# A transformer block's first image: LN1 tokens kept in the large buffers, weights loaded behind the first tokens and prepared in two stages, and a new order of the instructions

## The chip, the core and the metric

The kernel runs on one core of a Trainium2 chip. A core has five engines with an instruction queue each: TensorE (PE, matrix products and transposes), VectorE (DVE), ScalarE (ACT), GpSimd (POOL) and SyncE (SP, which here only issues transfers). Each works through its own queue in order; they wait for each other by semaphores. Transfers (DMA) are issued from the queues of SP, ACT and POOL. Data lie in SBUF (128 partitions) and, for PE's results, in eight PSUM banks. The metric is the device time of one execution in microseconds (us).

## What is computed

Sixteen images of 128 channels, 96 x 96 pixels, float32, go through one block: a layer norm over channels (LN1), channel attention with 8 heads, a residual sum, a second layer norm (LN2) and a feed-forward part with a depthwise 3x3 convolution, and a second residual sum. The reference, cut to what matters:

```python
xn1 = _layernorm(x_hwc, ln1_w, ln1_b)
q, k, v = xn1 @ wq.T, xn1 @ wk.T, xn1 @ wv.T         # 8 heads of 16 channels
q, k = _l2norm(q), _l2norm(k)                          # over all 9216 pixels
attn = softmax(einsum('bhcn,bhdn->bhcd', q, k) * 16 ** -0.5)
x = x + (attn applied to v) @ wp.T
xn2 = _layernorm(x, ln2_w, ln2_b)
h1 = einsum('bchw,oc->bohw', xn2, w_in)                # 128 -> 512 channels
h2 = depthwise_conv3x3(h1, w_dw)
x = x + einsum('bchw,oc->bohw', gelu(h2), w_out)       # 512 -> 128
```

## The kernel before

**Tiling.** An image is cut into 8 bands of 12 rows and 24 units of 4 rows (384 pixels). A band of x (128 channels x 1152 pixels) is one buffer of the pool `xb` or `x1`. Normalising needs pixels on partitions: 128 pixels form a tile, four tiles a *quad*; an image has 18 quads.

**LN1 and the Gram matrix** (`norm`, with `second` false). For each quad PE transposes four tiles (`forth`, line 602) into a PSUM bank (`h` for the first image, `tr` else), DVE takes their statistics (line 609), POOL computes variance plus epsilon (616) and its power -1/2 (620), and the tokens are scaled into a buffer `zT` (634 by DVE for half of the first image's tiles, 647 by ACT). There are three `zT` buffers, each with a column of ones. From `zT` PE sums the Gram matrix of the image (`gram`, 661) and transposes back to channels (`back`, 692, one bank `pB`), and ACT copies the result into a padded buffer `xn` (`place`, 698). A `zT` buffer is free for a later quad when its Gram product and its transposes back are done.

**Attention** (`attention`) works on the 128 x 128 Gram matrix alone: a chain of small steps on PE (764 to 846), DVE, POOL (810) and ACT (exp at 825), whose last result is one matrix `mwT`. PE then multiplies the normalised image by it (`mix`, 560), and x is added, by DVE (`residual`, 566) for the first image's first bands and otherwise by ACT (569) and an accumulating transfer (572).

**LN2** is `norm` again with `second` true: transposes (602), statistics, variance, power, the shift `nb` on DVE (624), scaling (638, 651), transposes back and place (696, with border rows at 702).

**Feed-forward.** For each band and each chunk of 128 hidden channels PE computes `hidden` (877), ACT copies it out (`kept`, 882), and the nine taps of the convolution are shared: ACT multiplies two or three taps into `pr` buffers (890) that accumulating transfers add (899), DVE does the others (895). For chunk 3 of about half the bands PE does the convolution as nine matmuls (945). Gelu follows on ACT (903, 951), then the output matmuls (968), DVE's sum (975) and the store (979). The large buffers `h3` (ten of them, 128 x 1152) hold the convolution's results; at the start two of them hold the raw weights.

**Weights** (`weights`). One step issues five loads on ACT's queue (417 to 421) into two `h3` buffers. PE transposes and DVE scales them into their final places: first those of attention (432 to 467), then the others (`winT`, `woutT`, `comp`).

**The order** is not written by hand. Every step is handed to `Plan.op` with its engine, an assumed duration, what it reads and writes, and a *place*, which is a position on the time line in units of feed-forward jobs plus an offset from the table `AT`, by kind of step. `Plan.order` plays the queues through with the assumed durations: when an engine is idle it takes, of the steps whose inputs are ready and whose buffers are free, that with the smallest place. The resulting sequence is what the program contains; on the chip each engine runs its part of it in that fixed order. Buffers of the pools in `IN_TURN` are given out in order of place. `T_ADD`, `T_MOVE` and `T_WEIGHTS` are the assumed durations of transfers; they act through the order alone.

Of the kernel before, what the change touches and what calls it, by code (L numbers as in the profile page):

```python
# [9 lines left out]
F32 = mybir.dt.float32  # L10
# [8 lines left out]
BR = 12  # L19
# [13 lines left out]
AT = dict(  # L33
    weights=86, zeros=34, load_a=-17.95, forth_a=-1.35, stats_a=-23.85, variance_a=50.15, power_a=-16.45,
    scaled_a=6.1, gram=-31.8, back_a=-145.85, place_a=68, attention=-19.55, mix=-17.6, residual=60.15,
    mixed=-98.2, add_x=-22.85, forth_b=-2, stats_b=-5.55, variance_b=52.05, power_b=-11, shift_b=-76.95,
    scaled_b=98.5, back_b=-23.15, place_b=20.55, halo=21.65, hidden=1.35, kept=-79.55, products=8.4,
    add_last=-64.4, tap=0.1, add_first=-14.5, gelu=-63.5, conv=1.15, conv_gelu=-1.85, out=4.9, add=-43.45,
    store=47.1,
)  # L40
# [4 lines left out]
WAIT = dict(POOL=350, SP=1300, ACT=1300)  # L45
T_WEIGHTS = 20000
T_VARIANCE = 420
T_POWER = 1000
T_ADD, T_MOVE = 3100, 1800

# [156 lines left out]
def tile_restormer_block(  # L207
# [138 lines left out]

    def at(kind, place):
        return place + AT[kind]

# [21 lines left out]
    def pe(ns, p, f, r, w):  # L371
        op("PE", ns, p, f, r, w, ns + 200 + SLACK, ns)
# [32 lines left out]
    def weights(p):  # L405
# [16 lines left out]

        def transposed(parts, kept, gives):

            key = ("weights", next(names))
            h = ("h", key)
            d = {}

            def forth():
                d["pt"] = bank(key)  # L430
                for k, part in enumerate(parts()):
                    nc.tensor.transpose(d["pt"][:, k * P : (k + 1) * P], part, ident)

            pe(440, at("weights", p), forth, mine, [h])
            dve(700, at("weights", p), lambda: kept(d["pt"]), [h], [("w", g) for g in gives] + mine[1:])

# [55 lines left out]
        def unit_parts():  # L492
            for n in range(NCH):
                nc.vector.tensor_scalar(v["wt"][:, n, :], v["win"][:, n, :], unit[:, n : n + 1], None, ALU.mult)

        op("ACT", 400, at("load_a", p), loads, [], mine, T_WEIGHTS, dma=2 * T_MOVE)
        dve(1400, at("weights", p), units, [], [("w", "in")])
        dve(400, at("weights", p), shifts, [], [("w", "in"), ("w", "conv"), ("w", "shift")])
        transposed(
            lambda: [v["wqk"][:, :P], v["wqk"][:, P:], v["wp"], wv_sb], keep_qkp, ["qk"]  # L500
        )
# [4 lines left out]
        dve(800, at("weights", p), keep_centred, [pc], [("w", "qk")])  # L506
        dve(700, at("weights", p), unit_parts, [mine[0], ("w", "in")], [mine[1]])
        transposed(
            lambda: [v["wt"][:, n, :] for n in range(NCH)],
            lambda pt: nc.vector.tensor_scalar(winT.rearrange("p n c -> p (n c)"), pt, w2, None, ALU.mult), ["in"],  # L510
        )
        transposed(
            lambda: [v["wout"][:, n * P : (n + 1) * P] for n in range(NCH)],
            lambda pt: nc.vector.tensor_copy(woutT.rearrange("p n c -> p (n c)"), pt), ["out"],
        )
        for t0 in (0, 4, 8):
            ts = range(t0, min(t0 + 4, 9))
            dve(170 * len(ts), at("weights", p), lambda ts=ts: comp_parts(ts), [mine[0]], [mine[1]])
            transposed(
                lambda ts=ts: [v["wt"][:, t % 4, :] for t in ts],  # L520
                lambda pt, ts=ts: nc.vector.tensor_scalar(
                    comp[:, ts[0] : ts[-1] + 1, :].rearrange("p t c -> p (t c)"), pt[:, : len(ts) * P],
                    w2, None, ALU.mult,
                ), ["conv"],
            )
# [18 lines left out]
    def norm(i, second, place_of):  # L544
# [8 lines left out]
        def x2(s, u):  # L553
# [22 lines left out]
            if loaded:  # L576
                pe(t_mm(UT), at("mix", s), mix, [*ins, xtok(u)], [pm])
                dve(t_dve(UT), at("residual", s), residual, [pm], [xtok(u)])
                return
            pe(t_mm(UT), at("mix", s), mix, ins, [pm, xtok(u)])  # L580
            act(t_act(UT, 1) - 43, at("mixed", s), mixed, [pm], [xtok(u)])
            if u % UPB == UPB - 1:
                xb = [xtok(b * UPB + k) for k in range(UPB)]
                add(at("add_x", s), add_x, [], xb)

        def pixels(s, m):
# [4 lines left out]
            key_ = "h" if early else "tr"  # L591
            by_dve = QT // 2 if early else 0

            def forth(q):
# [31 lines left out]
            def zT(q):  # L626
                zTs[q] = zT_bufs[plan.slot["zT", (name, q)]]
                return zTs[q]
# [38 lines left out]
            for q, tr in zip(qs, trs):  # L667
                units = {t // TPU: None for t in range(q * QT, (q + 1) * QT)}
                pe(110 * QT, at("forth" + ab, s), lambda q=q: forth(q), [xtok(u) for u in units], [tr])
            for j in range(QB * QT // 2):  # L670
                dve(341, at("stats" + ab, s), lambda j=j: stats(j), [trs[2 * j // QT]], [bt])
            op("POOL", T_VARIANCE, at("variance" + ab, s), variance, [], [bt], T_VARIANCE + 33 + SLACK)
            op("POOL", T_POWER, at("power" + ab, s), power, [], [bt], T_POWER + 33 + SLACK)
            if second:
                dve(80, at("shift" + ab, s), shift, [], [bt])
            for h, (q, tr) in enumerate(zip(qs, trs)):
                zt, sh = ("zT", (name, q)), s + STEP["scaled"] * h
                if by_dve:
                    dve(by_dve * 240, at("scaled" + ab, sh), lambda q=q: also_scaled(q), [tr, bt], [(*zt, 0)])
                act((QT - by_dve) * (343 if second else 250), at("scaled" + ab, sh), lambda q=q: scaled(q), [tr, bt], [(*zt, 1)])  # L680
                if not second:
                    pe(QT * 220, at("gram", sh), lambda q=q: gram(q), [(*zt, 0), (*zt, 1), ("w", "ones")], [("g", i)])

        def channels(s, u):
# [26 lines left out]
            quads = {(u * TPU + j) // QT: None for j in range(TPU)}  # L711
            pe(110 * TPU, at("back" + ab, s), back, [("zT", (name, q), k) for q in quads for k in range(2)], [pb])
            act(t_act(UT, 1) - 43 if second else t_copy(UT), at("place" + ab, s), place, [pb, ("w", "shift")], [z_unit(i, u)])
            for k, r, row, of in copies:
                act(225, at("place" + ab, s), lambda k=k, r=r, row=row: place_row(k, r, row), [pb, ("w", "shift")], [("z", k, of)])

# [242 lines left out]
    def ffn_out(p, g, s):  # L959
# [12 lines left out]

        def add():
            xt = x_unit(xbs, i, s + b * UPB)
            nc.vector.tensor_add(xt, d["po"], xt)  # L975
# [5 lines left out]
        for k, n in enumerate(order):  # L981
            pk = p + STEP["out_part"] * k
            pe(t_mm(UT), at("out", pk), lambda k=k, n=n: product(k, n), [("h3", (g, n), s), ("w", "out")], [po])
        dve(t_dve(UT), at("add", p), add, [po], [("xb", (i, b), s)])
        if g == NG - 1:
            move(at("store", p), lambda: store(s, 1), [("xb", (i, b), s)], [], T_MOVE / UPB)
        elif s == UPB - 1:
            move(at("store", p), lambda: store(0, UPB), [("xb", (i, b), k) for k in range(UPB)], [], T_MOVE)

# [63 lines left out]
```

## Time and profile before

| | |
|---|---|
| runs | 4176.35 us median of 3 (4175.98 to 4178.71) |
| profiled execution | 4194.94 us, span 4193.2 us |
| mean granted TensorE clock | 0.998 |
| DMA queue of POOL (accumulating transfers) | 82.9% of 16 engines' span |
| largest hardware DMA queue (loads of x, stores) | 9.8% |
| longest waits of PE | 5.6 us for the first x; 4.2 us for the first scaled tokens |

The span runs from the first to the last instruction of the profiled execution. A line of the timeline has the start and the busy time in us, the engine, the source line, the operation with what it writes and reads, and how many instructions are merged; in brackets is the idle time before it and who ended it. Busy times of neighbouring matmuls overlap, since they are pipelined. The granted clock is the share of full speed that TensorE was given.

### The profile page before, as it was taken

To read this page: it belongs to the slowest core of one execution; us is meant where nothing else is said; L and a number is where in the kernel's file an instruction comes from. 1 tells how busy PE (TensorE), PEld (TensorE's weight loads), DVE (VectorE), ACT (ScalarE), POOL (GpSimd) and SP (SyncE) were. 2 spreads that over 40 slices of the span, in tenths; PEclk is the share of its full clock that TensorE was granted. 3 is DMA by queue.
4 is the path that set the end of the run, shared out by engine and by line. 5 is a ranking of instruction groups with operands and counts; after the bars stand their busy time and mean duration, and the time that the engine had idled before them with its cause. 6 is when DMAs were issued, how large, how long until landed. Compare 5 with 4: busy or idle time off the path is not lost. (4 is left out here: it accounts for less than half of the span.)

```text
span 4193.2 us, 52283 instructions
## 1 busy us (share of the span) xinstructions
PE 4151.7 (99%) x17457; PEld 2684.0 (64%) x17457; DVE 4073.2 (97%) x4676; ACT 3682.0 (88%) x6970; POOL 2593.8 (62%) x2373
## 2 busy tenths in 40 slices
PE   8999999999999999999999999999999999999999
PEld 6666666666666666666666666666666666666565
DVE  6999999999999999999999999999999999999998
ACT  4988989899899888999988899898998989889885
POOL 3656666566675666657666566656656667565542
PEclk9999999999999999999999999999999999999999
DMA  2999999999999999999999999999999999999997
GB/s 78 192 191 201 208 198 208 189 213 201 206 207 204 206 196 204 203 202 207 198 206 198 197 206 198 206 201 201 208 197 212 195 207 202 191 205 199 196 197 160
DMA packets 203934, 827.63 MB, mean 197 GB/s; under 512 B 23568, under 2 KB 24976, under 8 KB 203664
## 3 DMA queue, kind: packets, MB, share of 16 engines
q0 software_dynamic: 164160, 672.47, 82.9%
q1 hardware_dynamic: 37152, 151.01, 9.8%
q8 instruction: 138, 2.26, 0.2%
q10 hardware_dynamic: 2352, 0.81, 0.1%
q14 instruction: 132, 1.08, 0.1%
HBM read 148.26 MB, written 75.50 MB: 53 GB/s over the span
## 5 line engine op out<-in xcount | busy, mean ns | idle before, releaser
L895 DVE SCALAR_TENSOR_TENSOR h<-h,ratio,h 128x1152 f32<-128x1152 f32 x2104 | 2933.0, 1415 | 5.0
L890 ACT ACTIVATE pr<-h,ratio 128x1152 f32<-128x1152 f32 x1018 | 1304.2, 1290 | 21.8 <-DMA pr<-pr 20.3
L945 PE MATMUL h<-xn,comp 128*128 128x384 f32 x3564 | 1277.4, 486 | 1.7 <-ACT h L951 0.9
L968 PE MATMUL h<-h,woutT 128*128 128x384 f32 x3072 | 1112.8, 487 | 1.8 <-ACT h L903 0.7
L877 PE MATMUL h<-xn,winT 128*128 128x384 f32 (+1 forms) x2676 | 1048.4, 500 | 2.1 <-DVE x L975 1.1
L945 PEld LDWEIGHTS h<-xn,comp 128*128 128x128 f32 x3564 | 647.3, 189 | 394.4 <-issue 10.4
L899 POOL DMA_DIRECT2D pr<-pr x573 | 545.7, 960 | 475.1 <-ACT pr L890 325.7
L968 PEld LDWEIGHTS h<-h,woutT 128*128 128x128 f32 x3072 | 560.7, 190 | 345.1 <-issue 7.5
L882 ACT COPY h<-h 128x384 f32<-128x384 f32 (+1 forms) x1338 | 658.1, 521 | 139.7 <-PE h L877 122.4
L877 PEld LDWEIGHTS h<-xn,winT 128*128 128x128 f32 x2676 | 479.5, 190 | 290.9 <-issue 49.7
L899 POOL DMA_DIRECT2D h<-pr x445 | 433.9, 977 | 356.7 <-DVE h L895 93.7
L895 DVE SCALAR_TENSOR_TENSOR h<-h,ratio 128x1152 f32<-128x1152 f32 x446 | 630.1, 1419 | 11.5 <-ACT h L882 7.8
L903 ACT ACTIVATE h<-h 128x1152 f32<-128x1152 f32 x448 | 533.7, 1192 | 51.9 <-DMA h<-pr 48.0
L616 POOL TENSOR_SCALAR ve_b<-st_b 128x4 f32<-128x4 f32 x288 | 364.3, 1265 | 310.8 <-DVE st_b L609 304.6
L620 POOL TENSOR_TENSOR rstd_b<-ve_b,mhalf 128x4 f32<-128x4 f32 x288 | 525.1, 1823 | 13.9
L620 POOL TENSOR_TENSOR rstd_a<-ve_a,mhalf 128x4 f32<-128x4 f32 x288 | 498.2, 1730 | 15.7 <-POOL ve_a L616 0.2
L616 POOL TENSOR_SCALAR ve_a<-st_a 128x4 f32<-128x4 f32 x288 | 323.9, 1125 | 292.2 <-DVE st_a L609 291.7
L651 ACT ACTIVATE zT<-pT_b,nb_b,rstd_b 128x128 f32<-128x128 f32 x1132 | 431.4, 483 | 45.7 <-DVE nb_b L624 45.4
L647 ACT ACTIVATE zT<-pT_a,rstd_a 128x128 f32<-128x128 f32 x1080 | 314.7, 398 | 39.3 <-POOL rstd_a L620 38.4
L661 PEld LDWEIGHTS g<-zT 128*128 128x128 f32 x2304 | 294.4, 192 | 50.0 <-ACT zT L647 7.9
L661 PE MATMUL g<-zT 128*128 128x129 f32 x2304 | 307.1, 276 | 3.3 <-ACT zT L647 3.3
L560 PE MATMUL h<-xn,mwT 128*128 128x384 f32 x768 | 283.5, 490 | 1.2 <-ACT x L569 0.8
(172 smaller groups left out, 3605.4 us busy)
## 6 DMA issues: line engine op xcount, KB each, us to landing
pr<-pr POOLq DMA_DIRECT2D x573, 576.0 KB, 6.9
h<-pr POOLq DMA_DIRECT2D x445, 576.0 KB, 7.4
x<-in_x_dram SPq DMA_DIRECT2D x128, 576.0 KB, 6.5
out_dram<-x SPq DMA_DIRECT2D x127, 576.0 KB, 5.6
x<-in_x_dram POOLq DMA_DIRECT2D x122, 576.0 KB, 7.7
out_dram<-x SPq DMA_DIRECT2D x3, 192.0 KB, 1.9
weights<-in_L_conv_w_in_dram ACTq DMA_DIRECT2D x1, 256.0 KB, 10.7
weights<-in_L_conv_w_out_dram ACTq DMA_DIRECT2D x1, 256.0 KB, 11.6
```

Of the source, the lines that this page charges most:

```text
L616: nc.gpsimd.tensor_scalar(ve, d["mv"][:, :, 2], 1.0 / C, EPS, ALU.mult, ALU.add)
L620: nc.gpsimd.tensor_tensor(rstd, d["ve"], mhalf, ALU.pow)
L651: nc.scalar.activation(zT(q)[:, k, :P], d["pT", q][:, k, :], AF.Identity, bias=d["nb"][:, t : t + 1], scale=d["rstd"][:, t : t + 1],)
L661: nc.tensor.matmul(grams[i][:, : P + 1], lhsT=zt[:, :P], rhs=zt, start=(q == 0 and k == 0), stop=(q == NU * TPU // QT - 1 and k == QT - 1),)
L877: nc.tensor.matmul(rows(ph), lhsT=winT[:, n, :], rhs=window(xn, r0 + r, e - r, 1), start=True, stop=True)
L882: nc.scalar.copy(window(h1_, r, e - r, 1), rows(d.pop(("ph", r))))
L890: nc.scalar.activation(to, shifted(t), AF.Copy, scale=ratio[:, n, t : t + 1])
L895: nc.vector.scalar_tensor_tensor(h3, shifted(t), ratio[:, n, t : t + 1], onto, ALU.mult, ALU.add)
L899: nc.gpsimd.dma_start(out=to, in_=d["pr", t], accum_op=ALU.add)
L903: nc.scalar.activation(h3, h3, AF.Gelu)
L945: nc.tensor.matmul(d["pc"], lhsT=comp[:, t, :], rhs=window(xn, r0 + dy, UR, dx), start=(t == 0), stop=(t == 8),)
L968: nc.tensor.matmul(rows(d["po"]), lhsT=woutT[:, n, :], rhs=h3s[g, n][:, s * UR : (s + 1) * UR, :], start=(k == 0), stop=(k == NCH - 1),)
```

## The change

The first image's LN1 gets its token buffers from the pool `h3`: two quads share one large buffer, so that its 18 quads need nine buffers and none waits for one of the three `zT` buffers. The columns of ones in them are set on POOL, before each pair of quads. LN2 and all other images use the three `zT` buffers as before. The weights' loads have a place of their own (`load_w`), and the preparation of `winT`, `woutT` and `comp` has another (`late`) than that of attention's weights (`weights`). Most kinds of steps of the first image get their own offset (names ending in `_0`), all offsets are new, and so are three assumed durations. No step computes anything else, and the number of instructions is the same but for 18 small memsets. (`add` is renamed `add_here`.)

```diff
 AT = dict(
-    weights=86, zeros=34, load_a=-17.95, forth_a=-1.35, stats_a=-23.85, variance_a=50.15, power_a=-16.45,
-    scaled_a=6.1, gram=-31.8, back_a=-145.85, place_a=68, attention=-19.55, mix=-17.6, residual=60.15,
...
+    load_w=20.7, weights=-42.35, zeros=-138.3, load_a=-151.9, forth_a=0.1, stats_a=-36.15, variance_a=263.5,
+    power_a=249.55, scaled_a=74.15, gram=2.55, back_a=-28.75, place_a=112.3, attention=-146.85, mix=-33.95,
...
+    add_first=-120.05, gelu=196.55, conv=2.95, conv_gelu=9.4, out=6.5, add=-10, store=164.8, mix_0=-40.75,
+    residual_0=378.9, mixed_0=-198.6, add_x_0=-364.75, gram_0=9.85, forth_a_0=-6.55, forth_b_0=2.65,
+    stats_a_0=-99.05, stats_b_0=-205.9, scaled_a_0=-81.4, scaled_b_0=247.4, back_a_0=-172.15, back_b_0=-50.5,
+    place_a_0=-98.9, place_b_0=-35, shift_b_0=-201.25, late=-145.5,
 )
-T_WEIGHTS = 20000
+T_WEIGHTS = 12000
-T_ADD, T_MOVE = 3100, 1800
+T_ADD, T_MOVE = 3060, 1640
...
-    def at(kind, place):
-        return place + AT[kind]
+    def at(kind, place, i=1):
+        return place + AT[kind if i else kind + "_0"]
...
-        op("ACT", 400, at("load_a", p), loads, [], mine, T_WEIGHTS, dma=2 * T_MOVE)
+        op("ACT", 400, at("load_w", p), loads, [], mine, T_WEIGHTS, dma=2 * T_MOVE)
...
-        dve(700, at("weights", p), unit_parts, [mine[0], ("w", "in")], [mine[1]])
+        dve(700, at("late", p), unit_parts, [mine[0], ("w", "in")], [mine[1]])
...
+            apart = i == 0 and not second
...
             def zT(q):
-                zTs[q] = zT_bufs[plan.slot["zT", (name, q)]]
+                if q in zTs:
+                    return zTs[q]
+                if not apart:
+                    zTs[q] = zT_bufs[plan.slot["zT", (name, q)]]
+                    return zTs[q]
+                two = [k for k in (q - q % 2, q - q % 2 + 1)]
+                t = h3p.tile([P, BR * W], F32, tag="h3", name=f"zT_{two[0]}")
+                for k in two:
+                    zTs[k] = t[:, k % 2 * QT * (P + 1) : (k % 2 + 1) * QT * (P + 1)].rearrange("p (t c) -> p t c", c=P + 1)
+                    nc.gpsimd.memset(zTs[k][:, :, P:], 1.0)
                 return zTs[q]
...
-                zt, sh = ("zT", (name, q)), s + STEP["scaled"] * h
+                zt, sh = zt_of(q), s + STEP["scaled"] * h
                 if by_dve:
+                    if apart and q % 2 == 0:
+                        both = [(*zt_of(k), j) for k in (q, q + 1) for j in range(2)]
+                        op("POOL", 200, at("zeros", sh), lambda q=q: zT(q), [], both, 300)
...
+        def zt_of(q):
+            return ("h3", ("zT", q // 2), q % 2) if i == 0 and not second else ("zT", (name, q))
```

## The prediction

> **What bounds the kernel now.** I read the engines' totals first, then the timeline of TensorE (PE), then stretches of it. The totals name two full engines:
>
> ```profile
> span 4193.2 us, 52283 instructions
> ...
> PE 4151.7 (99%) x17457; PEld 2684.0 (64%) x17457; DVE 4073.2 (97%) x4676; ACT 3682.0 (88%) x6970; POOL 2593.8 (62%) x2373
> ```
>
> A matmul's busy time overlaps its neighbours', so "99%" isn't yet work. The timeline gives the real pitch, from one start to the next (columns: start, busy, engine, line, operation, count):
>
> ```profile
> 39.90 0.60 PE L602 MATMUL h<-ident,x 128*128 128x128 f32 x4
> 40.34 1.06 PE L661 MATMUL g<-zT 128*128 128x129 f32 x8
> 41.23 0.49 PE L692 MATMUL pB_a<-ident,zT 128*128 128x128 f32 x3
> ...
> 4174.00 15.64 PE L968 MATMUL h<-h,woutT 128*128 128x384 f32 x48
> ```
>
> A transpose takes (40.34-39.90)/4 = 0.11 us, a Gram matmul 0.89/8 = 0.111, and a 384-column matmul (15.64-0.49)/47 = 0.322. The six L877 matmuls from 101.22 to 103.48 (four of 480 columns, two of 384) give 0.40 for 480 columns. The groups by shape count 9640 of 384 columns (3109 us), 440 of 480 (177), 4629 transposes (509), 2304 Gram matmuls (256) and some 54 us of small ones. PE's work is thus about 4105 us, its last matmul ends at 4189.6, and 85 us are lost. I cut the span at PE's first hidden matmul, first tap matmul, first output matmul, and the attention ends of images 1 and 15 (columns: stretch, length, PE busy and count, granted clock, DMA share, GB/s):
>
> ```profile
> 0.00:92.02 92.02, 75.65 (x494) 0.94 0.27 87
> 92.02:103.48 11.46, 11.46 (x47) 1.00 0.00 0
> 103.48:147.03 43.55, 37.96 (x171) 0.97 0.84 177
> 147.03:261.68 114.65, 114.65 (x494) 0.98 0.95 204
> 261.68:3854.64 3592.96, 3576.94 (x15124) 1.00 0.96 202
> 3854.64:4189.64 335.00, 335.00 (x1135) 1.00 0.89 186
> ```
>
> With each instruction at its pitch, PE's work up to these six ends is 62.8, 74.2, 110.0, 221.4, 3770.1 and 4104.5 us. So the stretches lose 29.2, 0.1, 7.8, 3.2, 44.3 and 0.6 us. The last line shows that PE can run with nothing lost, to the end. The work of all engines stays as it is (only 18 small memsets are added), so the change can move these 85 us and no others. VectorE's (DVE) work, made the same way (a tap 1.33, a 256-wide stats 0.335, an add 0.47), is 4040 us. It is the second bound, some 65 us behind PE.
>
> **The start in detail.** PE waits for x until 5.6, then for the first scaled tokens:
>
> ```profile
> 13.47 0.73 PE L692 MATMUL pB_a<-ident,zT 128*128 128x128 f32 x2 [4.22 <-DVE zT L634]
> 15.49 0.48 PE L692 MATMUL pB_a<-ident,zT 128*128 128x128 f32 x1 [1.29 <-ACT zT L647]
> 15.76 3.24 PE L661 MATMUL g<-zT 128*128 128x129 f32 x16
> 18.84 0.49 PE L692 MATMUL pB_a<-ident,zT 128*128 128x128 f32 x3
> 19.17 0.60 PE L602 MATMUL h<-ident,x 128*128 128x128 f32 x4
> ```
>
> After 19 LN1 is PE-bound: a quad is 4 transposes, 8 Gram matmuls and 4 transposes back, 1.77 us, and quads mostly follow every 1.66 to 1.8. The rest of the 29.2 goes in attention (51.17 to 66.88 holds 9.0 us of PE work) and from the first mix to the first hidden matmul (66.88 to 92.02 holds 19.9).
>
> **The change, part by part.** *Tokens in the large buffers.* The three zT buffers tied a Gram product to the transposes back. In the new instruction order quad 4's transposes stand ahead of the first Gram product, so they can go when ScalarE (ACT) has scaled quad 0, at 15.07+0.6 = 15.7 instead of 19.17. From there to quad 8's transposes stand 6.3 us of PE work (four quads forth at 0.44, Gram 0 to 3 at 0.89, back 1 to 3 at 0.33), which would end at 22.0.
>
> *Weights loaded later on ACT's queue.* Five DMA issues move from 5.67, where ACT had nothing to do until 13.78, to behind the third place copy (about 19.6). Their rows are 0.35+0.51+0.33+0.45+0.52 = 2.16 us. Behind them on ACT stands quad 4's scaling, then on PE quad 8's transposes: 19.6+2.2+0.6, at 22.4 to 22.6. Before, those started at 25.16 with Gram 4 and back 4 and 5 (1.55 us) done in addition, so like with like 23.6. Gain 1.0; bounds 0 (the row from 6.06 to 7.40 shows an issue held up by 0.9 us) and 3.4 (19.17-15.7). The weights' longest landing is 11.6 us, so they are there by 19.6+2.2+11.6 = 33.4; PE asks for them near 42. That cover is 9 us; if it goes, attention is late by the same amount. The x loads on SP lose their company in the DMA engines, but PE waited for x only once, at 5.6.
>
> *Eighteen memsets* at 0.04 each (L394 rows) push `ident` on POOL by 0.7 us, to about 2.4; x arrives at 5.57. Nothing, with 3 us of cover.
>
> *Two-stage weights and attention.* The work before attention's first matmul is 33.7 instead of 33.9: -0.2. On ACT, a whole quad of image 1 (1.14) and a place copy (0.48) now stand ahead of the copy of u, which has about 1 us of room: +0.6. At the end, mix stood behind a Gram product (65.74 to 66.88) though its matrix was there at 65.6; now only three back and four forward transposes stand there, and the matmul on y lost its four: -1.4. Sum -0.8, bounds -2.0 (also the 0.3 at softmax and the 0.4 ahead of L791) and +1.2 (the second ACT item costs in full). First mix at 66.88-1.0-0.2-0.8 = 64.9.
>
> *Mix to hidden.* By the order, PE's work up to the first mix is 44.1 (was 42.9) and up to the first hidden matmul 66.9 (was 62.8): three more quads of image 1 forth and back, two more Gram products. So 22.8 us of work instead of 19.9 in a stretch that lost 5.2. The additions fall where PE waited 1.96 for DVE and for banks. I take 3.2 lost; bounds 1.0 and 5.2. Hidden starts at 64.9+22.8+3.2 = 90.9. The loss by then is 24.0 instead of 29.2, a **gain of 5.2**; bounds 0.2 and 11.
>
> *First tap.* DVE would have to follow. Before, it idled here, as ACT copied out two hidden chunks and then did other work:
>
> ```profile
> 97.33 1.42 DVE L895 SCALAR_TENSOR_TENSOR h<-h,ratio 128x1152 f32<-128x1152 f32 x1 [4.43 <-ACT h L882]
> ```
>
> Now three copies stand in a row: tap at 90.9+2.25+0.7 = 93.9, with 56.1 us of DVE work done instead of 54.1. DVE gains 5.4, so the PE gain isn't stopped there. At the first output PE is still 3.8 us of work further (113.8).
>
> *New order, images 1 to 15.* No row prices this. The planner's constants act only through the order. I counted, in both orders, how often PE comes back to one of the four `h` banks with under 2 us of its own work between: 163 before, 104 now. For the one `pB` bank it is 111 and 112. Of the 44.3 lost, 16.0 show as idle (3592.96-3576.94). I take a tenth, -4.4. Bounds: -16.0 (all that shows) and +16 (as much again, nearest to the images' spread: one image loses between 0.8 and 6.7). The 7.8 after the first tap I leave; bounds -5 and +4.
>
> Sum: -5.2-4.4 = -9.6. The profiled execution's 4194.9 (span 4193.2 and 1.7 around it) becomes 4185.3. It lies 18.6 above the median shown, so on the median's scale 4176.35-9.6 = **4166.8**.
>
> [...] In the start the granted clock (fourth column) falls to half:
>
> ```profile
> 54.00:56.00 2.00, 2.00 (x17) 1.00 0.00 0
> 56.00:58.00 2.00, 2.00 (x12) 0.50 0.64 136
> 64.00:66.00 2.00, 2.00 (x12) 0.50 0.50 88
> 78.00:80.00 2.00, 2.00 (x7) 0.53 0.00 0
> ```
>
> Over 56 to 80 this takes 5.1 us of matmul time. I count none of it as gained, since the first fall comes after two microseconds without any idle. [...]
>
> **Rivals.** *R1, the start's gain is given back.* DVE is 97% busy and near full from 110 on; if the three early quads only make `tr` banks and POOL wait later, the steady order gives nothing. For: PE lost 7.8 us at 103 to 147 with ACT 86 to 100% busy in 100 to 140. Against: DVE gains as much as PE. Time: between no change and 5.2 gained, 4173.
>
> *R2, much more.* PE keeps its clock (5.1) and the new order takes a third of the 44.3 (14.8): 4176.35-5.2-5.1-14.8 = 4151. For: the last image runs with 0.6 lost, and a third fewer short bank reuses. Against: `pB` is as tight as before.
>
> *R3, slower.* One mechanism: LN2's shift on DVE (L624) waits for POOL's power (L620), and taps queue behind it. It waits 35 times, 38.3 us; the path from the last stats to the shift was 5.0 us at 2005.56 to 2010.57. DVE's own work between them is 4.85 us on average in the old order and 4.70 in the new, under 6 us in 254 cases instead of 236. If those waits double, DVE idles 38.3 more; DVE idled about 80 in the long stretch where PE lost 44.3, so 0.55 of it reaches PE: +21-5.2, 4192. It decides (8.35 slower) from some 23 more such waits. Against: cases under 4 us fall from 79 to 69.
>
> **From cases to numbers.** 0.2% of 4176.35 is 8.35 us, about what a measurement of this kernel can tell from no change. Forecast 0.42 (its own range 4159 to 4172; 0.36 of it below 4168.0), R1 0.22 (0.02 faster, 0.20 same), R2 0.14 (faster), R3 0.22 (slower). Faster 0.52, same 0.26, slower 0.22. The range reaches half into R2 and half into R3: 4149 to 4188.
>
> **What would show it.** Quad 4's transposes near 15.7 and quad 8's near 22.5; first mix near 65, first hidden matmul near 91, first tap near 94; PE's loss up to the first hidden matmul at 24; in the long stretch about 40 lost. The forecast is wrong if ACT's DMA issues hold LN1 for more than 3 us, if first hidden comes after 95, or if the wait of DVE's shift (L624 before) for POOL rises well above 38 us.

## The result, and the profile after

Beside the kernel before on the same chip, the changed kernel took 4171.04 us (median of 22 runs, 4167.26 to 4176.01), the kernel before 4176.23 (4173.82 to 4182.56): ratio **0.9986**, 95% interval 0.9980 to 0.9993. A second measurement, in the experiments, gave 0.9990 (0.9982 to 0.9999). So the change gains 4 to 6 us, under the 0.2% (8.35 us) that the prediction counts as a change.

The profiled execution took 4175.62 us. Its totals, from the page:

```profile
span 4173.9 us, 52446 instructions
...
PE 4142.5 (99%) x17457; PEld 2679.6 (64%) x17457; DVE 4070.0 (98%) x4676; ACT 3693.7 (88%) x6970; POOL 2479.5 (59%) x2391
```

The span is 19.3 us shorter than in the profile before, though the medians differ by 5.2. That is the first riddle, and cutting the span shows where the 19.3 lie. Of the changed kernel, cut at PE's first hidden matmul, first output matmul, and the attention ends of images 1 and 15 (columns: stretch, length, PE busy and count, granted clock, DMA share, GB/s):

```profile
0.00:91.95 91.95, 77.21 (x531) 0.98 0.29 93
91.95:145.72 53.77, 50.27 (x209) 0.97 0.73 151
145.72:248.69 102.97, 101.24 (x427) 1.00 0.93 197
248.69:3833.54 3584.85, 3577.33 (x15159) 1.00 0.96 203
```

With each instruction at the pitch that the prediction uses, PE's work up to these four ends is 66.9, 113.8, 212.7 and 3768.7 us. The losses are 25.1, 6.8, 4.1 and 28.8. The long stretch lost 44.3 before; here it loses 15.5 less, far more than the runs gained.

Three views of the start. PE in LN1 (columns: start, busy, engine, line, operation, count, idle before and its releaser):

```profile
13.40 0.73 PE L714 MATMUL pB_a<-ident,zT 128*128 128x128 f32 x2 [4.23 <-DVE zT L650]
...
15.69 1.10 PE L609 MATMUL h<-ident,x 128*128 128x128 f32 x4
16.59 1.93 PE L677 MATMUL g<-zT 128*128 128x129 f32 x8
18.31 0.85 PE L714 MATMUL pB_a<-ident,zT 128*128 128x128 f32 x3
18.95 1.06 PE L609 MATMUL h<-ident,x 128*128 128x128 f32 x4
...
25.62 0.63 PE L609 MATMUL h<-ident,x 128*128 128x128 f32 x4 [0.95 <-DVE zT L650]
```

Quad 4's transposes stand at 15.69, where they were predicted, but the four take 0.90 us to the next start and the eight Gram matmuls 1.72 (18.31-16.59), twice their later pitch. Quad 8's transposes come at 25.62; 22.5 was predicted. ACT at that time:

```profile
21.71 0.48 ACT L720 COPY xn<-pB_a 128x384 f32<-128x384 f32 x1 [1.51 <-PE pB_a L714]
21.72 0.35 ACTq L420 DMA_DIRECT2D weights<-in_L_conv_wq_dram  x1
22.11 0.45 ACTq L421 DMA_DIRECT2D weights<-in_L_conv_wk_dram  x1
22.65 0.39 ACTq L422 DMA_DIRECT2D weights<-in_L_conv_wp_dram  x1
23.08 0.45 ACTq L423 DMA_DIRECT2D weights<-in_L_conv_w_in_dram  x1
23.56 0.52 ACTq L424 DMA_DIRECT2D weights<-in_L_conv_w_out_dram  x1
24.13 0.63 ACT L663 ACTIVATE zT<-h,rstd_a 128x128 f32<-128x128 f32 x2 [1.93 <-DMA weights<-in_L_conv_wk_dram]
```

The five issues stand in a row from 21.72 to 24.08, and quad 4's scaling waits behind them. And VectorE, at the very start:

```profile
7.85 0.17 DVE L487 TENSOR_SCALAR unit<-dw 128x4 f32<-128x4 f32 x1 [6.79 <-DMA dw<-in_L_conv_w_dw_dram]
...
10.18 0.16 DVE L482 TENSOR_TENSOR b<-b,none 128x1 f32<-128x1 f32 x1
10.26 0.75 DVE L616 BATCH_NORM_STATS2 st_a<-h 128x6 f32<-128x256 f32 x2
```

The first statistics start at 10.26, though PE's first transposes began at 5.52: small operations on the tap weights `dw` and the shifts stand ahead of them in DVE's queue and wait for a DMA until 7.85. The kernel before has the same queue (10.33). The prediction did not see it.

Attention's first matmul comes at 51.69 (51.17 before), the first mix at 66.69, the first hidden matmul at 91.95. DVE's first tap follows with a shorter wait than the 4.43 us before:

```profile
95.32 1.42 DVE L917 SCALAR_TENSOR_TENSOR h<-h,ratio 128x1152 f32<-128x1152 f32 x1 [2.88 <-ACT h L904]
```

### The profile page after: what moved, and what is told of

It reads as the page before. It is cut to its first block, busy times and chain, and to the rows that moved or that the text cites. A ratio compares the mean times of both kernels' runs of the same rounds, so it can differ in the third digit from the quotient of the medians.

```text
span 4173.9 us, 52446 instructions
## 1 busy us (share of the span) xinstructions
PE 4142.5 (99%) x17457; PEld 2679.6 (64%) x17457; DVE 4070.0 (98%) x4676; ACT 3693.7 (88%) x6970; POOL 2479.5 (59%) x2391
## 4 chain that ended last, share of the span: by engine, by line
PE 88%; DVE 4%; DMA 3%; ACT 3%; POOL 1%; issue 1%; ACTq 0%; POOLq 0%; DVEq 0%
PE h L967 25%; PE h L990 21%; PE h L899 19%; PE g L677 5%; PE h L566 5%; DVE h L917 3%; PE pB_b L714 3%; PE pT_b L609 3%; PE pB_a L714 3%; PE pT_a L609 2%; DMA h<-pr 2%; DMA pr<-pr 1%; ACT pr L912 1%; ACT h L904 0%; DVE st_a L616 0%
## 5 line engine op out<-in xcount | busy, mean ns | idle before, releaser
L990 PE MATMUL h<-h,woutT 128*128 128x384 f32 x3072 | 1137.1, 486 | 1.0 <-ACT h L904 0.4
L899 PE MATMUL h<-xn,winT 128*128 128x384 f32 (+1 forms) x2676 | 1078.6, 500 | 1.1 <-ACT h L904 1.0
L921 POOL DMA_DIRECT2D pr<-pr x573 | 562.6, 989 | 493.2 <-ACT pr L912 385.7
L904 ACT COPY h<-h 128x384 f32<-128x384 f32 (+1 forms) x1338 | 667.9, 520 | 182.0 <-PE h L899 162.1
L921 POOL DMA_DIRECT2D h<-pr x445 | 424.7, 956 | 531.5 <-DVE h L917 119.0
L925 ACT ACTIVATE h<-h 128x1152 f32<-128x1152 f32 x448 | 536.0, 1198 | 17.0 <-DMA h<-pr 13.9
L627 POOL TENSOR_TENSOR rstd_a<-ve_a,mhalf 128x4 f32<-128x4 f32 x288 | 534.4, 1856 | 12.7
L627 POOL TENSOR_TENSOR rstd_b<-ve_b,mhalf 128x4 f32<-128x4 f32 x288 | 506.8, 1760 | 11.3
L623 POOL TENSOR_SCALAR ve_b<-st_b 128x4 f32<-128x4 f32 x288 | 293.8, 1020 | 219.8 <-DVE st_b L616 204.8
L623 POOL TENSOR_SCALAR ve_a<-st_a 128x4 f32<-128x4 f32 x288 | 276.8, 961 | 226.0 <-DVE st_a L616 211.8
```

The costliest lines, as they stand in the source:

```text
L623: nc.gpsimd.tensor_scalar(ve, d["mv"][:, :, 2], 1.0 / C, EPS, ALU.mult, ALU.add)
L627: nc.gpsimd.tensor_tensor(rstd, d["ve"], mhalf, ALU.pow)
L899: nc.tensor.matmul(rows(ph), lhsT=winT[:, n, :], rhs=window(xn, r0 + r, e - r, 1), start=True, stop=True)
L904: nc.scalar.copy(window(h1_, r, e - r, 1), rows(d.pop(("ph", r))))
L921: nc.gpsimd.dma_start(out=to, in_=d["pr", t], accum_op=ALU.add)
L925: nc.scalar.activation(h3, h3, AF.Gelu)
```

## The experiments

Kernels with the same median in brackets were measured side by side and share the runs of the kernel before. "Lost" is PE's time less its work at the pitches of the prediction: up to the first hidden matmul, from there to image 1's attention end, and from there to image 15's (one profiled execution each; extra transposes are not counted as work). The ratio is taken over all runs, so it can differ a little from the quotient of the medians. The profiled execution need not lie at the median: that of the extra transposes is the fastest of its eleven runs (4167.34 beside 4173.24), and the first of the changed kernel lies 4.6 us above its median.

| kernel | median (before) us | ratio, 95% interval | lost to first hidden | to image 1 | to image 15 |
|---|---|---|---|---|---|
| before, profile shown first | | | 29.2 | 11.1 | 44.3 |
| changed, first profile | 4171.04 (4176.23) | 0.9986, 0.9980 to 0.9993 | 25.1 | 10.9 | 28.8 |
| before again | 4179.16 (4179.78) | 0.9999, 0.9990 to 1.0008 | 27.9 | 10.8 | 27.1 |
| new start alone | 4193.43 (4179.78) | 1.0037, 1.0024 to 1.0049 | 28.6 | 15.9 | 38.4 |
| old start, new rest | 4179.60 (4179.78) | 1.0003, 0.9994 to 1.0012 | 29.7 | 10.1 | 26.1 |
| weight loads on SyncE | 4173.03 (4179.78) | 0.9989, 0.9980 to 0.9997 | 24.7 | 10.1 | 26.8 |
| small zT buffers | 4181.26 (4178.88) | 1.0005, 0.9996 to 1.0014 | 32.0 | 10.2 | 25.9 |
| second stage late | 4178.49 (4178.88) | 1.0000, 0.9991 to 1.0008 | 27.9 | 10.2 | 26.6 |
| tap weights wait, order follows | 4183.32 (4178.88) | 1.0013, 1.0004 to 1.0022 | 27.9 | 11.5 | 29.3 |
| extra transposes | 4173.24 (4178.88) | 0.9989, 0.9980 to 0.9998 | 23.6 | 8.9 | 24.6 |
| changed again | 4172.75 (4177.01) | 0.9990, 0.9982 to 0.9999 | 25.0 | 9.7 | 27.0 |
| tap weights moved, order kept | 4168.75 (4177.01) | 0.9980, 0.9971 to 0.9989 | 22.1 | 9.7 | 28.6 |
| the same, loads on SyncE | 4166.77 (4177.01) | 0.9977, 0.9968 to 0.9986 | 20.2 | 10.8 | 27.3 |
| the same, transposes and table early | 4169.60 (4177.01) | 0.9982, 0.9973 to 0.9991 | 14.9 | 9.0 | 35.2 |

**Both kernels once more.** No edit.

> The kernel before, unchanged, for a second profile. The prediction took its steady terms from one execution (4194.94 us) that lies 18.6 us over the median of its timed runs. Theory A (about 15 us of the 44.3 us that TensorE lost between the first attention of image 1 and the last attention belonged to that one execution): a profiled execution near the median shows 28 to 33 us lost in that stretch and the same 29 us before the first hidden matmul. Theory B (the loss of 44.3 us is the kernel's own, and the median hides nothing): 41 to 47 us again. Both expect a time ratio of 1.000 within 0.001.

> The changed kernel, unchanged, for a second profile and a second timing beside the three below. Theory A (the gain is made ahead of the first attention of image 1 and is 3 to 6 us; the steady order gives nothing): ratio 0.9985 to 0.9995; TensorE loses 24 to 26 us before the first hidden matmul and 27 to 30 us between the first attention of image 1 and the last. Theory B (its first timing was a lucky chip): ratio 0.9995 to 1.0005.

Measured: Theory A in both, with the kernel before a little below its ranges (27.9 lost up to the first hidden matmul, 27.1 in the long stretch). The kernel before, second profile, with its cuts at its own first hidden and output matmuls and attention ends (columns as above; PE's work is 62.8, 110.0, 221.4 and 3770.1):

```profile
0.00:90.70 90.70, 73.88 (x493) 0.98 0.27 88
90.70:145.71 55.01, 49.57 (x217) 0.97 0.67 140
145.71:260.11 114.40, 114.40 (x494) 0.98 0.95 205
260.11:3835.95 3575.84, 3568.95 (x15123) 1.00 0.96 203
```

The long stretch holds 3575.84 us for 3548.7 of work: 27.1 lost, not 44.3. The busy column says it too: idle time there is 6.9 us (3575.84-3568.95) where the first profile had 16.0. So 17 us of the loss that the prediction shared out belonged to one execution: 4194.94 us, where the highest of the 115 runs of this kernel in the brackets above is 4186.08. DVE's wait for POOL, on which the slower rival was built, shrinks with it; from the waits of DVE (total us, times, longest), before again and then changed:

```profile
DVE nb_b L624 <- POOL rstd_b L620: 22.7, 24, 2.0
```

```profile
DVE nb_b L631 <- POOL rstd_b L627: 22.7, 22, 2.8
```

38.3 us in 35 waits was that first execution's, too. Between like executions the two kernels wait the same.

**The two halves apart.** The table of places was split, so that the first image looks up one and all else the other:

```diff
-    def at(kind, place, i=1):
-        return place + AT[kind if i else kind + "_0"]
+    def at(kind, place, i=1):
+        return place + (AT[kind] if i else AT0.get(kind + "_0", AT0[kind]))
...
+AT0 = (changed places)   AT = (places before)      # new start alone
+AT0 = (places before)    AT = (changed places)     # old start, new rest
```

So that the planner can place every step, the mixtures are not exact. In the new start alone `load_w` is 17.0 instead of 20.7, and the old T_ADD and T_MOVE are back; in the old start the loads of x, the attention's place and image 0's mix and second norm are the changed kernel's, and the old T_WEIGHTS is back.

> The start of the changed kernel (LN1 of image 0 in the large buffers, weights early and in two stages, its own places for all steps of image 0's two norms and its attention), and the places of the kernel before for everything else, the FFN's steps of image 0 among them. Theory A (the whole timed gain of 5.2 us is made before the first hidden matmul): 4171 to 4173 us, about -4 against the kernel before; TensorE loses about 25 us before the first hidden matmul. Theory B (the new steady order gives the gain and the start gives its part back): 4175 to 4177 us.

> The counterpart: the first norm of image 0 and the weights as in the kernel before (three small token buffers, weights prepared in one stage and late), and the changed kernel's places for the second norm of image 0, for all later images and for the FFN. Theory A (the start makes the gain): 4175 to 4177 us, TensorE loses about 29 us before the first hidden matmul. Theory B (the steady order makes it): 4170 to 4172 us. If the two act apart, this ratio and that of the new start alone multiply to 0.9986.

Measured: the old start behaves as Theory A says: first hidden matmul with 29.7 lost, ratio 1.0003. The changed order of images 1 to 15 gives nothing by itself that can be told from noise (26.1 lost in the long stretch, 27.1 with the order before). The new start alone fits neither theory: 4193.43 us. It loses 15.6 us between the first output matmul (129.01) and image 1's attention end, and 13.9 more in the next image; the changed kernel loses 4.1 and 2.9 there. So the two do not act apart, and this pair cannot price the start. In these two stretches of its profile TensorE's granted clock stands at 0.50 from 233.17 to 240.00 and from 287.78 to 298.02, 17.1 us in all, which is at most 8.5 of the 29.5 us lost. What the mixed order waits for first in image 1 stays open.

**What the start is made of.** Two parts undone, one at a time:

```diff
-            apart = i == 0 and not second
+            apart = False
...
-            return ("h3", ("zT", q // 2), q % 2) if i == 0 and not second else ("zT", (name, q))
+            return ("zT", (name, q))                 # small zT buffers
...
-    late=-145.5,
+    late=86,                                         # second stage late
```

> The changed kernel with one part undone: the normalized tokens of image 0's LN1 lie in the three small buffers again; all places as in the changed kernel. Theory A (in the first 30 us LN1 waits for VectorE's statistics, TensorE's half pitch and ScalarE, not for buffers): attention's first matmul at 51.5 to 52.5 us (51.7 with the large buffers), time within 1 us of the changed kernel, 4170 to 4172 us. Theory B (the buffers are what makes the start): quad 4's transposes back at about 19 us in place of 15.7, attention's first matmul at 53 us or later, 4173 to 4176 us.

> The changed kernel with the second stage of the weights (winT, woutT, comp) put back at the low place that the weights had before (86 in place of -145.5); loads and first stage stay early. Theory A (the early second stage is cover: its transposes fill TensorE's waits of the attention and let the mix and the first hidden matmul come without a gap): attention's stretch loses 1 to 2 us more, TensorE loses 27 to 28 us before the first hidden matmul in place of 25, and the time is 4172 to 4174 us. Theory B (the second stage is hidden either way): 4170.5 to 4171.5 us.

Measured: without the large buffers attention's first matmul comes at 55.89 and the first hidden one at 98.91; the ratio is 1.0005. Theory B is right that the gain goes (by more than it expected) and wrong about the way. Quad 4's transposes stay at 15.59: the new places bring them forward, not the buffers. With three buffers the plan instead pushes weight work into LN1, 36.2 us of PE work ahead of attention instead of 33.7, and attention, with less left to lay over it, loses 7.9 us up to its end instead of 4.0. The late second stage meets Theory A: 27.9 lost up to the first hidden matmul, ratio 1.0000, the whole gain gone (a bit more than expected). So each part alone, undone, takes all of the gain: with the large buffers work stays out of LN1, and the early second stage lays it over the attention. Both edits also made the planner draw up a new order for all engines, so what each part is worth in an unchanged order is not shown.

**What holds LN1.** Three waits were taken away one at a time from the changed kernel:

```diff
-            nc.scalar.dma_start(out=v["wqk"][:, :P], in_=wq)
+            nc.sync.dma_start(out=v["wqk"][:, :P], in_=wq)
...
-        dve(1400, at("weights", p), units, [], [("w", "in")])
+        dve(1400, at("weights", p), units, [z_unit(0, 1)], [("w", "in")])
...
+            def warm(n):
+                for _ in range(n):
+                    nc.tensor.transpose(grams[i][:, 3 * P :], ident, ident)
```

The first line stands for all five loads (and the step's engine is SyncE). The second also hands `weights` to the plan behind the first norm. The third is called with 12 ahead of quad 0's transposes and with 24 behind quad 3's.

> The changed kernel with the five early weight loads issued by SyncE in place of ScalarE. Theory A (these issues, 21.7 to 24.1 us on ScalarE, hold the zT quads behind them, and so the transposes of quad 8, which came at 25.6 us where 22.5 was predicted): quad 8's transposes come at 23 to 24 us, attention's first matmul at 49.7 to 50.7 us in place of 51.7, and the time falls by 1 to 2 us against the changed kernel (4169 to 4170 us). Theory B (TensorE's half pitch from 15.7 to 21.2 us and VectorE set it): attention's first matmul at 51.2 to 51.9 us, 4171 us.

> The changed kernel with VectorE's eleven small operations on the tap weights and the shifts (2.5 us, 7.85 to 10.33 us, behind the DMA of dw) made to wait until image 0's second unit is placed, so that the first statistics no longer stand behind them. Theory A (this queue on VectorE, which both kernels have, is what the large buffers could not shorten): the first statistics start at 6.3 to 6.8 us in place of 10.26, the first transposes back at 10 to 11 us in place of 13.4, attention's first matmul at 48.5 to 50 us in place of 51.7, and 1 to 3 us of the time are gained over the changed kernel (4168 to 4170 us). Theory B (a gain before the attention is eaten inside it, as with the weight loads moved to SyncE, where 2.25 us earlier left 0.4 us at the first hidden matmul): the attention begins as early as Theory A says, the first hidden matmul comes within 0.6 us of 91.95, and the time stays at 4170 to 4172 us.

> The changed kernel with 36 extra transposes of the identity into unused PSUM columns: 12 ahead of image 0's first transposes and 24 behind its sixteenth, in TensorE's idle time at the start. Theory A (TensorE's half pitch at 5.5 to 9.2 us and 15.7 to 21.2 us comes from its idle time before): the four transposes of quad 4 take about 0.6 us in place of 1.10 and the eight Gram matmuls behind them about 1.06 in place of 1.93; LN1 gains 2 to 2.7 us, attention's first matmul at 49 to 50 us. Theory B (the half pitch belongs to the data or to the first use of the buffers): 1.10 and 1.93 us as before, attention's first matmul at 51.5 to 52 us.

Measured. *Loads on SyncE:* attention's first matmul at 49.44, as Theory A says (quad 8's transposes, at 24.35, a little later). At the first hidden matmul 0.4 us are left, and the ratio, 0.9989, is the changed kernel's. The gain is made in LN1 and gone behind the attention; the attention's stretch up to its end loses 5.8 us instead of 4.0. *Tap weights waiting:* attention's first matmul at 46.64, 5 us earlier, yet the first hidden one at 95.95, 4 us later; ratio 1.0013. Neither theory: the plan drew up another order for all engines, with 68.1 us of PE work ahead of the first hidden matmul instead of 66.9, and lost 8.0 us up to the attention's end, then 6.2 up to the first hidden matmul and 10.2 up to the first output (changed: 4.0, 3.2 and 6.8). *Extra transposes*, PE in the profile:

```profile
2.22 2.82 PE L606 MATMUL g<-ident 128*128 128x128 f32 x12 [2.22 <-POOL ident masks.py:199]
...
7.70 2.78 PE L606 MATMUL g<-ident 128*128 128x128 f32 x24
13.46 0.59 PE L725 MATMUL pB_a<-ident,zT 128*128 128x128 f32 x2 [2.98 <-DVE zT L661]
15.49 0.36 PE L725 MATMUL pB_a<-ident,zT 128*128 128x128 f32 x1 [1.44 <-ACT zT L674]
15.74 1.12 PE L618 MATMUL h<-ident,x 128*128 128x128 f32 x4
```

The first twelve take 0.235 us each, the 24 behind them 0.116. Then PE idles 2.98 and 1.44 us, and quad 4's four transposes are slow again, 1.12 us (0.66 in the third start below). The numbers are Theory B's, its cause isn't: the time of one and the same operation on the same data falls from 0.235 to 0.116. The granted clock of this run changes with the pitch (columns: stretch, length, PE busy and count, granted clock, DMA share, GB/s):

```profile
12.24:15.65 3.41, 0.75 (x3) 1.00 1.01 414
15.65:19.06 3.41, 3.41 (x17) 0.50 0.13 54
19.06:22.50 3.44, 3.44 (x33) 1.00 0.08 24
```

Behind 3.41 us with 0.75 us of work the clock falls to half at 15.65, just ahead of quad 4's transposes, and comes back at 19.06, where a transpose goes from 0.21 to 0.11 us. The 24 end at 10.48, 5.2 us ahead of the fall, and attention's first matmul stays at 51.59; ACT's issues end at 23.98 here, too.

**The order kept.** The tap weights' operations were then cut into five and issued between the statistics and the scalings of quads 2, 4, 6, 8 and 10, with the plan unchanged, so that only DVE's queue differs:

```diff
-        dve(1400, at("weights", p), units, [], [("w", "in")])
+        dve(1400, at("weights", p), lambda: None, [], [("w", "in")])
...
             def also_scaled(q):
+                if apart and q in TAP_AFTER:
+                    staged["tap_part"](TAP_AFTER.index(q))
```

> The changed kernel with VectorE's small operations on the tap weights and shifts split in five and put between the statistics and the scalings of quads 2 to 10 of LN1, with no other instruction of any engine in another order (the version before let the order change with it). Theory A (once the order stays, an earlier LN1 is kept): first transposes back at 10.3 us in place of 13.4, attention's first matmul at 48.5 to 50.5 us, first hidden matmul at 89.5 to 91 us in place of 91.95, time 1 to 2.5 us under the changed kernel. Theory B (the weights' loads on ScalarE, or the work laid over the attention, eat it): first hidden matmul at 91.4 to 92.2 us, time within 0.7 us of the changed kernel.

> The same, and the five weight loads issued by SyncE in place of ScalarE. Theory A (the two waits of LN1 stood one behind the other and both go): attention's first matmul at 46 to 47.5 us, first hidden matmul at 88 to 90 us, time 2 to 4 us under the changed kernel. Theory B (the attention's chain and TensorE's order inside it eat it): attention's first matmul as early, first hidden matmul at 91 us or later, time within 1 us of the changed kernel.

> The same as the one before, with two more things for the start: 20 extra transposes of the identity on TensorE (12 ahead of the first transposes, 8 behind the sixteenth) against its half pitch, and one small activation ahead of ScalarE's DMA issues, so that its table load (1.28 us at 13.7 us, ahead of the first zT) is done early. Theory A (each of these waits stands on LN1's chain): the first zT of ScalarE 1.3 us earlier, quad 4's four transposes in about 0.6 us in place of 1.1, attention's first matmul at 43.5 to 45.5 us, time 3 to 6 us under the changed kernel. Theory B (absorbed behind the attention as before): time within 1 us of the one before.

The second kernel adds the loads on SyncE. The third adds 12 and 8 extra transposes and

```diff
+    early_act = const.tile([P, 1], F32, name="early_act")
+    nc.scalar.activation(early_act, ones, AF.Copy, scale=1.0)
```

Measured: with the order kept the gain stays. Attention's first matmul at 48.85, the first hidden one at 88.96 (2.9 earlier than in the changed kernel's second profile), image 1's attention end 2.9 earlier too, time 4168.75, 4.0 us under the changed kernel beside it: Theory A, with more time gained than it expected. With the loads on SyncE, DVE's first operations read

```profile
6.48 0.43 DVE L621 BATCH_NORM_STATS2 st_a<-h 128x6 f32<-128x256 f32 x1 [5.43 <-PE h L614]
...
14.56 0.15 DVE L481 TENSOR_SCALAR unit<-dw 128x4 f32<-128x4 f32 x1
```

and the first hidden matmul comes at 87.09, time **4166.77**, ratio 0.9977 (0.9968 to 0.9986): 6 us under the changed kernel, the best of all here. Theory A, beyond its ranges for the first hidden matmul and the time.

The third start is the fastest by far. PE, in its profile:

```profile
8.40 1.04 PE L613 MATMUL g<-ident 128*128 128x128 f32 x8
10.01 0.59 PE L734 MATMUL pB_a<-ident,zT 128*128 128x128 f32 x2 [0.57 <-DVE zT L670]
...
11.01 0.66 PE L625 MATMUL h<-ident,x 128*128 128x128 f32 x4
11.50 1.06 PE L697 MATMUL g<-zT 128*128 128x129 f32 x8
```

With gaps under 0.6 us PE keeps its pitch (0.12 for quad 4's transposes; eight Gram matmuls 0.90). The first hidden matmul comes at 81.82, 10 us ahead of the changed kernel, image 1's attention end at 236.68, 7.0 ahead of the kernel with loads on SyncE. The time, 4169.60, is 3.15 us under the changed kernel, as Theory A has it, but not under the kernel without the third edit (the intervals overlap). The lead shrinks in the long stretch, shown first with and then without that edit:

```profile
236.68:3827.85 3591.17, 3579.54 (x15159) 1.00 0.97 203
```

```profile
243.70:3827.05 3583.35, 3576.72 (x15158) 1.00 0.96 203
```

PE idles 11.6 us there instead of 6.6 and loses 35.2 instead of 27.3. No single wait carries it (DVE's shift waits 25.7 us for POOL in this stretch instead of 21.2, the rest is spread). Unlike the first profile of the kernel before, this execution is no outlier: it took 4169.86 us, and the median of its runs is 4169.60. So the lead of 7.0 us at image 1's attention end is given back in an ordinary execution; by what stays open.

## Why the prediction came out as it did

It said 4166.8; the median is 4171.0, inside the range and inside the case called likeliest (4159 to 4172). But the gain is too small for its own bound, where it held a gain above that bound to be likelier. Of the 9.6 us forecast 5.2 came, or 4.3 in the second measurement; that the number still lies in the range is owed to the range's width (4149 to 4188). Step by step:

*New order, images 1 to 15: -4.4. Wrong, and this step makes the difference of 4.2.* The working took a tenth of the 44.3 us lost. The second profile of the kernel before loses 27.1 there, the changed kernel 28.8 and 27.0, and the changed order without the new start gains nothing (1.0003). "About 40" became 28, but from 27. The prediction had noticed that the profile lay 18.6 us above the median and corrected the sum for it, yet not the terms taken from that profile. The first rival's premise (the steady order gives nothing) held, and its 4173 is nearer to 4171.0 than the forecast; no run shows the way that it gave for this (DVE near full, `tr` banks and POOL waiting later).

*The start: -5.2. Right in sign and place, a bit large.* Lost up to the first hidden matmul: 29.2 and 27.9 before, 25.1 and 25.0 after, so 2.9 to 4.2 gained; up to image 1's attention end 40.3 and 38.8 against 36.0 and 34.8, on average 4.1, which is about what the runs show.

*LN1: -1.0. Missed.* Attention's first matmul was to come at about 50.0 and came at 51.69 and 51.63. The step put the five DMA issues at 19.6; they began at 21.72, because PE ran at half pitch (0.214 us a Gram matmul) up to 20.66 us and the third place copy came late. What the profile before showed in 19.17 to 20.5 at 0.11 us a transpose or Gram matmul was carried over to work that starts earlier, where they took 0.22. The prediction's own lines had the sign of it: sixteen Gram matmuls from 15.76 to 18.84 take 0.19 us each, not 0.111. Taking the issues away gave 49.44. And the larger wait of LN1 the prediction had not seen at all: DVE's queue from 7.85 to 10.26, which both kernels have.

*Attention: -0.8.* First matmul to first mix took 15.0 us (before 15.7 and 14.9), now with 10.4 us of work in it instead of 9.0. The loss is 4.6 instead of 6.7 and 5.9: the gain lies in the work laid over it. *Mix to hidden:* 2.5 and 2.4 lost, 3.2 predicted, 5.3 and 4.1 before. Right in kind; the experiment with the late second stage suggests what fills it.

*First tap at 93.9:* 95.32, late with the hidden matmuls; DVE follows, as said. *The 7.8 us after it,* left as they were: 6.8 and 5.8.

*The clock: no gain.* Right for the falls between 56 and 80 us that were counted. In the first profile before, three of them cost 5.1 us. The second profile before shows one at 60 to 65 (1.7 us), the changed kernel one (columns as in the first cuts):

```profile
61.80:65.20 3.40, 1.55 (x11) 1.00 0.37 144
65.20:68.60 3.40, 3.40 (x11) 0.50 0.29 60
68.60:70.00 1.40, 1.40 (x6) 1.00 0.67 277
```

Here the fall lasts 3.40 us and at a clock of 0.50 costs 1.7 us, and the 3.40 us ahead of it had 1.85 us of idle PE. In the first profile before, the 3.41 us ahead of the fall at 56.00 hold only 0.42 us of idle PE, so these rows show no idle time that the falls have in common. The rival "much more" counted three falls (5.1 us) and a third of the 44.3 as saved. That more work for PE keeps the clock was not shown, and the kernel before, in a second execution, has one of the three falls. A later fall was not counted: near 140 us the clock is at 0.50 for 6.8 us in both profiles before and for 3.4 us in both of the changed kernel, at most 1.7 us of work. The kernel with the old start has the short one too and gains nothing (1.0003), so this is not shown to be part of the gain.

*Slower by POOL's wait:* did not come; 22.7 us in both kernels.

## What to carry to other kernels

Take the losses that are to be shared out from an execution near the median; one 18 us above it needs a second profile first, since a term taken from it can be that execution's own. Where a planner sets the order, an edit's price holds only if the order stays: a similar move of 2.5 us of work on VectorE cost some 10 us when the plan was redrawn (ratio 1.0013 against the changed kernel's 0.9986 and 0.9990), and gained 4 when only that queue was touched (0.9980). Before widening buffers at a kernel's start, read what stands first in each engine's queue: a small operation behind a late DMA, five DMA issues, and TensorE's half pitch with a table load of 1.28 us were worth 2.8, 2.2 and 3.7 us at attention's first matmul, one taken away after the other; the last of them did not shorten the time. Where TensorE starts slowly, read its pitch from start to start: the clock column cannot tell ahead of the trace's first entry (20.81 us in the changed kernel).

## What was not expected of the hardware

At the start TensorE runs at half its later pitch, and the clock column of the changed kernel's profile does not show it: the sixteen transposes at 5.52 take 3.65 us, 0.23 each, quad 4's transposes at 15.69 take 0.22 us each and the Gram matmuls behind them 0.215, yet this stretch (columns: stretch, length, busy time and count of PE, its weight loads, DVE, ACT and POOL, granted clock, DMA share, GB/s) shows full speed:

```profile
16.00:18.50 2.50, 2.50 (x13) 2.50 (x12) 1.67 (x6) 1.04 (x4) 0.95 (x3) 1.00 0.10 41
```

The 1.00 is no measurement here: the first clock entry of this trace, at full speed, begins at 20.81 us, and the column counts time without an entry as full. From one start to the next the Gram matmuls take 0.214 us up to 20.66 and 0.111 from 20.85 on, so the pitch changes at that entry. Where entries cover the same work, they say 0.50: from 15.65 to 19.06 with the extra transposes (rows above), and from 13.19 to 20.01 with the late second stage, whose quad 4's transposes, at 15.88, take 0.22 us each.

Behind idle gaps of 2.98 and 1.44 us with only two transposes between them the granted clock of the run with extra transposes was 0.50 from 15.65 on; in the third start, with gaps under 0.6 us, quad 4's transposes took 0.12 us each. The first twelve of the extra transposes took 0.235 us each; ahead of the first clock entry the profile says nothing of the clock (in the traces of the kernels before and after it begins at 18.45 and 20.81 us).

Issuing a weight load on ScalarE's queue in LN1 took 0.35 to 0.52 us of ScalarE's time each, once 1.16 us (in the kernel with extra transposes), and on a path with 1.66 us per quad five of them were felt: without them attention's first matmul came at 49.44 instead of 51.69.
